# Folding the weights of two layers on four row groups of TensorE, inside a phase of matmuls

## The chip, the cores and the metric

The kernel runs on one core of a Trainium2 chip. The metric is the device time of one execution in microseconds (us). A core has five engines with a queue of instructions each, which they work off in order: TensorE (PE, matmuls), VectorE (DVE), ScalarE (ACT), GpSimd (POOL) and SyncE (SP). DMAs are issued from the queues of SP and POOL here. PE writes to PSUM, whose banks hold 128 partitions of 512 fp32 values; DVE and ACT copy results from there to SBUF.

## What is computed

Four layers follow each other on x, of shape (1024, 16, 16, 16) in fp32 (batch, height, width, channels), each with a group normalisation ahead of it and a residual sum:

```python
x = x + _L0_conv_ref(_gn(x), L0_conv_core0, L0_conv_core1, L0_conv_core2)   # a tensor-train matrix
x = x + _L1_conv_ref(_gn(x), ...)   # a step of a neural cellular automaton
x = x + _L2_conv_ref(_gn(x), L2_conv_filters, L2_conv_bias)                 # a 3x3 convolution
x = x + _L3_conv_ref(_gn(x), ...)   # as layer 1, with other weights
```

Layers 1 and 3 are these, where each channel is filtered with the 3x3 windows `conv1_w` and `conv2_w` and the result goes through two dense layers:

```python
xt = jnp.transpose(x, (0, 3, 2, 1))
pre = _alive(xt)
y1 = _depthwise(xt, conv1_w, conv1_b)
y2 = _depthwise(xt, conv2_w, conv2_b)
flat = jnp.concatenate([xt, y1, y2], axis=1).reshape(B * W * Hh, 48)
h = jax.nn.relu(flat @ fc0_w.T + fc0_b)
d = (h @ fc1_w.T + fc1_b).reshape(B, C, W, Hh)
...
xn = (xt + d) * (pre & _alive(d))
```

The reshape to rows of 48 doesn't move the channels to the end. A row of 48 is therefore three consecutive lines of 16 values of an image plane, some of them from filtered planes. For such lines the kernel doesn't filter the input: it folds the filter into the first dense layer's weights ("weight folding"). The folding depends on weights alone and is done once per execution and layer.

## The kernel before

The batch is cut into two halves of 512, and a matmul works on [128 partitions] x [512 batch columns]. Two buffers of SBUF, X0 and X1, hold one half each of the activations.

**Layer 0** runs in five phases (`layer_train`). A unit of phase 1 has five products of four matmuls each, and every two of these matmuls (L1078) are one piece: ten pieces a unit, 16 units, 160 pieces in the phase. After the first piece of each unit, `build` (L989) makes the stationary weights of the next unit: sixteen passes (L1001) on four row groups into four PSUM banks `pw` of tag "w", of which there are four in all (L1477), and four ACT copies to SBUF (L1006). The products go into three banks of tag "o" and are taken out by DVE (L1112, L1114) and, for one product of a unit, by ACT (L1110). DVE also adds pairs of weights (L1019, "mix").

**Weight folding** (`nca_weights`, L220) makes, for each of layers 1 and 3, a list of steps: inputs, dense0, bias_lines, bias_rows, dense1, taps, order, xpats, and then the folds. Its scratch tiles lie in X1, which is free until the last quarter of the phase.

- `dense0` turns the weights of the first dense layer and stores them to DRAM as `fz`: for each of three lines 18 rows of 128 (the first and last are zero).
- `taps` (L319) collects the filter windows on DVE into `tk`, whose nine used rows stand at partitions 0 to 2, 32 to 34 and 64 to 66, and loads the shifted rows of `fz` from DRAM into `fs` with nine DMAs from POOL (L327). `fs` has 96 partitions and 2,048 columns.
- `order` (L332) spreads `tk` into `tp` with 20 POOL copies (L340) and writes rows of zeros to DRAM (L349, eight DMAs a layer).
- `xpats` (L309) loads, copies and stores another table (L314 to L317) from POOL.
- A fold (L359; eleven a layer) multiplies a column block of `tp` with `fs`, 2,048 columns in four matmuls (L382). `half` does two of them into one bank of tag "m", of which there is one, onto partitions 0 to 35 and 64 to 99, and two copies bring them to a staging tile `fold_e`; `evac` (L149) gives them to ACT and DVE in turn (L152, L154). There are two staging tiles a layer, used in turn. `send` (L390) then writes the fold to DRAM (`wy`) with 2 to 16 DMAs from POOL (L394), 160 in all.

**What sets the order.** The schedule is manual: each engine runs its instructions in the order in which the code issues them. `run` (L1423) issues the pieces of a phase and places background steps between them: a step is issued after the piece at which its planned share of the phase is reached. Here the background is `beside(make1, make3)` over the first 0.74 of phase 1 (L1501): a step of layer 1, a pause of 2.6, the same step of layer 3, a pause of 2.6, and then the pause of the list in L1471. If the pauses take more than 0.7 of the stretch, they are shrunk to that; the rest of the stretch is shared out among the steps:

```python
idle = sum(b[0] for b in bg if b[1] is None) / (us * (hi - lo))
less = min(1.0, 0.7 / idle) if idle else 1.0
```

A step may put instructions on several queues at once, behind all that is already in them. In the last quarter of the phase X1 is loaded for the next phase.

Of the kernel before, what the change touches and what calls it, by code (L numbers as in the profile page):

```python
# [18 lines left out]
B, S, C = 1024, 16, 16  # L19
P = 128  # L20
NB = 512
NCH = B // NB
NL = 32
HID = 128
# [21 lines left out]
TERMS = [  # L46
    ((0, 0),),
    ((0, 1),),
    ((0, 1), (1, 0)),
    ((0, 2), (1, 1)),  # L50
    ((0, 2), (1, 1), (2, 0)),
    ((1, 1), (2, 0)),
    ((1, 2), (2, 1)),
    ((2, 1),),
# [43 lines left out]
def channel(q, k, g):  # L98

    return 12 * q + 3 * ((k - g) % 4) + k  # L100
# [3 lines left out]
def conv_preact_kernel(ctx: ExitStack, tc: tile.TileContext, a: dict, out: bass.AP):  # L104
    nc = tc.nc
    V, A, G, T = nc.vector, nc.scalar, nc.gpsimd, nc.tensor
# [33 lines left out]
    def bank(shape, tag, name):  # L140
        p, sizes = pool["ps"]
        return p.tile(shape, F32, tag=tag, name=name, bufs=sizes[tag])

    def psum(shape, name):
        return bank(shape, shared[0], name)
# [3 lines left out]
    def evac(dst, src):  # L149
        flip[0] ^= 1  # L150
        if flip[0] and not on_vector[0]:
            A.copy(dst, src)  # L152
        else:
            V.tensor_copy(dst, src)  # L154
# [22 lines left out]
    for hf in range(2):  # L177
        rows = slice(64 * hf, 64 * hf + 64)
# [41 lines left out]
    def nca_weights(pre, room):  # L220
# [3 lines left out]
        fz = dram.tile([3, S + 2, HID], F32, tag=pre + "fz", name=pre + "fz")  # L224
# [5 lines left out]
        def tmp(rows, line, lo, n):  # L230
            return flat[0:rows, NB * line + lo : NB * line + lo + n]
# [3 lines left out]
        fc0t, fcb = tmp(16, 1, 0, 3 * HID), tmp(48, 2, 0, 3 * HID)  # L235
        ind = tmp(48, 3, 0, 768).rearrange("p (s r) -> p s r", s=3)

        fs = tmp(96, 5, 0, S * HID)
        tc3 = tmp(96, 2, 384, 96).rearrange("p (j k) -> p j k", k=3)
        tk = tmp(96, 9, 0, 32 * len(TERMS)).rearrange("p (n c) -> p n c", c=32)  # L240
        tp = tmp(96, 14, 0, 72 * len(TERMS)).rearrange("p (n f m) -> p n f m", f=2, m=36)
        pk = tmp(P, 10, 0, 833)
        fold_e = [tmp(P, 12, 0, 2 * NB), tmp(P, 3, 0, 2 * NB)]
        zero = tmp(32, 0, 256, HID)
        def inputs():
            G.dma_start(fc0n, a[pre + "fc0_w"])
            G.dma_start(fc1n, a[pre + "fc1_w"])
            G.dma_start(b0, a[pre + "fc0_b"].unsqueeze(1))
            V.memset(pk[:, 0:512], 0.0)
            V.memset(zero, 0.0)  # L250
            V.memset(ones, 1.0)
            V.memset(cb, 0.0)
            V.memset(ind, 1.0)
            for j in range(2):
                G.dma_start(
                    cb[16 * j + 16 : 16 * j + 32], a[pre + f"conv{j + 1}_b"].unsqueeze(1)
                )
            for m in range(2):
                G.dma_start(pk[16 * m : 16 * m + 16, 512:513], a[pre + "fc1_b"].unsqueeze(1))
            with nc.allow_non_contiguous_dma(reason="144 values"):  # L260
                for j in range(2):
                    for s in range(3):
                        G.dma_start(
                            tc3[32 * s : 32 * s + 3, 16 * j : 16 * j + 16],
                            a[pre + f"conv{j + 1}_w"].rearrange("c o i j -> j c (o i)"),
                        )
            V.memset(tk, 0.0)
            V.memset(tp, 0.0)
            V.memset(fs, 0.0)
            for s in range(3):  # L270
                for base, step in ((s, 1), (15 - s, -1)):
                    G.affine_select(
                        out=ind[:, s], in_=ind[:, s], pattern=[[3 * step, 256]], base=base,
                        channel_multiplier=-16 * step, compare_op=ALU.is_ge, fill=0.0,
                    )
# [43 lines left out]
        def taps():  # L319

            for n, terms in enumerate(TERMS):
                for s, kw in terms:
                    rows = slice(32 * s, 32 * s + 3)
                    V.tensor_copy(tk[rows, n], tc3[rows, :, kw])
            for s in range(3):
                for kh in range(3):
                    G.dma_start(  # L327
                        fs[32 * s + kh : 32 * s + kh + 1],
                        fz[s, 2 - kh : 18 - kh].rearrange("h k -> (h k)").unsqueeze(0),
                    )  # L330

        def order():  # L332

            for f in range(2):
                for k in range(3 - f):
                    for g in range(4):
                        qs = [q for q in (1, 2, 3) if channel(q, k, g) + f >= C]
                        c0 = channel(qs[0], k, g) + f - C
                        col = 12 * k + 4 * (qs[0] - 1) + g
                        G.tensor_copy(  # L340
                            tp[:, :, f, col : col + 4 * len(qs) - 3 : 4],
                            tk[:, :, c0 : c0 + 12 * len(qs) - 11 : 12],
                        )
            for n, pats in enumerate(TRIPLES):
                for i, pat in enumerate(pats):
                    for v in range(2):
                        if pat[v] is None:
                            for s in slots(n, i):
                                G.dma_start(  # L349
                                    wy.rearrange("q g v h s k -> v s (q g) h k")[v, s],  # L350
                                    zero[0:12].unsqueeze(1).broadcast_to([12, S, HID]),
                                )

        def slots(n, i):
            return [6 * k + 3 * n + i for k in range(3)] if n < 2 else [12 + 3 * n + i]
# [3 lines left out]
        def fold(n):  # L359

            steps = []
            for f in range(2):

                uses = []
                for m, pats in enumerate(TRIPLES):
                    for i, pat in enumerate(pats):
                        over = m == 2 and i > 0 or m == 3 and i > 1
                        if over == bool(f):
                            for v in range(2):
                                if pat[v] == n:  # L370
                                    ks = range(3) if m < 2 else [m - 2]
                                    uses += zip(ks, slots(m, i), [v] * 3)
                if not uses:
                    continue
                e = fold_e[turn[0]]
                turn[0] ^= 1

                def half(a2, f=f, e=e):
                    pe = psum([P, NB], pre + "pe")
                    for hh in range(2):  # L380
                        h0 = NB * (2 * hh + a2)
                        T.matmul(  # L382
                            pe[64 * hh : 64 * hh + 36], tp[:, n, f], fs[:, h0 : h0 + NB],
                            start=True, stop=True,
                        )
                    for hh in range(2):
                        rows = slice(64 * hh, 64 * hh + 36)
                        evac(e[rows, NB * a2 : NB * a2 + NB], pe[rows])

                def send(e=e, uses=uses):  # L390
                    for k, s, v in uses:
                        for hh in range(2):
                            r0 = 64 * hh + 12 * k
                            G.dma_start(  # L394
                                wy.rearrange("q g v h s k -> v s (q g) h k")[
                                    v, s, :, 8 * hh : 8 * hh + 8
                                ],
                                e[r0 : r0 + 12].rearrange("p (h k) -> p h k", h=8),
                            )

                steps += [lambda half=half: half(0), lambda half=half: half(1), send]
            return steps

        steps = [inputs, dense0, bias_lines, bias_rows, dense1, taps, order, xpats]
        return L, steps + [x for n in range(len(TERMS)) for x in fold(n)]


# [1061 lines left out]
    def beside(xs, ys):  # L1469

        pause = [12, 8, 1, 1, 6, 6, 4, 4] + [1] * (len(xs) - 8)  # L1471
        return [z for x, y, t in zip(xs, ys, pause) for z in (x, 2.6, y, 2.6, t)]

    L1, make1 = nca_weights("L1_conv_", X1[:, 0:16])
    L3, make3 = nca_weights("L3_conv_", X1[:, 16:32])
    with ExitStack() as es:
        stage(es, dict(gn, w=2, r=2, gq=2, R=1), dict(o=3, w=4, m=1))  # L1477
# [105 lines left out]
```

## Time and profile before

| | |
|---|---|
| median of three runs | 3199.57 us (3197.21 to 3203.37) |
| profiled execution, its own time | 3191.8 us |
| span of the profile | 3190.1 us |
| mean granted TensorE clock | 0.98 of full speed |
| phase 1 of layer 0 in the profile | 234.8 to 601.8 us |
| PE, DVE, ACT, POOL busy in 234.8 to 622 us (387.2 us) | 377.9, 212.3, 69.5, 164.4 us |
| matmul records of the folding (L382) | 176, first at 299.4, last at 517.0 us |

In the lines of the profile an instruction stands as its source line, engine and operation, then what it writes and reads ("out<-in"), with the number of partitions and elements. All scratch tiles of the folding appear as `xn`, since they lie in X1; its PSUM tiles are `L_conv_pe` and the like; its DRAM tables are `L_conv_fz`, `L_conv_wy` and `L_conv_pk`. PEld is TensorE's loading of stationary weights, which overlaps PE. One matmul in fp32 leaves two records, one for each pass. A timeline line gives the start, the time from there to the end of the last of the merged instructions, their number, and in brackets the idle time of the engine before them with what ended it. Ends of matmuls are modelled, so a record's length is longer than its share of PE: what a group costs is read from its start to the start of the next.

### The profile page before, as it was taken

The page shows a single profiled execution, that of the slowest core. Times are in us where ns is not written, and L with a number is a line of the kernel's source. Part 1 is how long each engine was busy: PE and PEld are TensorE (multiplying, and loading weights), DVE is VectorE, ACT ScalarE, POOL GpSimd, SP SyncE. Part 2 cuts the span into 40 slices and gives each one's busy share as a digit, 9 for nine tenths or more (in the row PEclk, how much of TensorE's full clock was granted, in tenths as well). Part 3 has the DMA queues.
Part 4 walks back from the last instruction along what each step waited for, and adds up shares of the span by engine and source line. Part 5 has one row for each costly group of instructions (what it writes and reads, how often), then busy time and mean ns, then how long its engine had stood idle before and what let it go on. Part 6 is the DMA issues. An engine that isn't in the chain of part 4 may idle for free.

```text
span 3190.1 us, 37179 instructions
## 1 busy us (share of the span) xinstructions
PE 3058.5 (96%) x13874; PEld 1260.3 (40%) x13874; DVE 1785.6 (56%) x2378; ACT 1018.3 (32%) x1690; POOL 670.6 (21%) x706
## 2 busy tenths in 40 slices
PE   7899899999999999999999999999979899999996
PEld 5444333444444444444444433333323233333332
DVE  5255345755554555544556678558757647754222
ACT  4331221100001000000111166666624356655553
POOL 1116532200000000000000034435432124432221
PEclk8999999999999999999999999999989999999998
DMA  7535545443333433322222254454476765433445
GB/s 283 201 142 97 121 101 160 133 144 104 104 109 132 146 116 104 104 98 96 90 95 90 76 168 133 129 167 154 139 192 110 185 139 173 136 92 115 128 137 186
DMA packets 243299, 424.77 MB, mean 133 GB/s; under 512 B 37844, under 2 KB 91952, under 8 KB 239408
## 3 DMA queue, kind: packets, MB, share of 16 engines
q1 hardware_dynamic: 217824, 368.63, 35.5%
q0 software_dynamic: 24480, 53.48, 8.3%
q8 instruction: 110, 1.80, 0.2%
q14 instruction: 69, 0.57, 0.1%
q10 hardware_dynamic: 816, 0.30, 0.0%
HBM read 238.78 MB, written 165.60 MB: 127 GB/s over the span
## 4 chain that ended last, share of the span: by engine, by line
issue 46%; PE 31%; POOL 8%; DMA 4%; DVE 2%; SPq 1%; ACT 1%; POOLq 0%; DVEq 0%; ACTq 0%
PE ph L1410 11%; PE po L1078 10%; PE po L1263 4%; POOL res L1313 4%; POOL u L1312 4%; PE po L1160 2%; DMA xn<-xf 1%; PE L_conv_pe L382 1%; SPq L941 1%; DVE xn L621 1%; DMA hx<-xn 1%; PE pw L1001 1%; PE ptout L948 1%; DVE sq L592 1%; POOL L_conv_wy L394 0%
## 5 line engine op out<-in xcount | busy, mean ns | idle before, releaser
L1078 PE MATMUL po<-xn,w 128*128 128x512 f32 x3584 | 1584.3, 598 | 4.6 <-DVE xn L892 4.6
L1078 PEld LDWEIGHTS po<-xn,w 128*128 128x128 f32 x3584 | 669.9, 190 | 852.6 <-issue 833.7
L1413 ACT ACTIVATE hid<-ph,pack 128x512 f32<-128x512 f32 x1024 | 653.9, 686 | 429.2 <-PE ph L1410 308.4
L1114 DVE TENSOR_TENSOR r<-r,po 128x512 f32<-128x512 f32 x576 | 377.8, 683 | 499.0 <-PE po L1078 476.3
L1312 POOL TENSOR_TENSOR u<-u,mask 128x512 f32<-128x512 f32 x128 | 202.5, 1582 | 1858.9 <-DMA nx<-xn 1241.7
L1410 PE MATMUL ph<-xn,wq 32*128 32x512 f32 x3664 | 573.1, 613 | 1.5 <-DMA wq<-L_conv_wy 1.5
L1006 ACT COPY w<-pw 128x512 f32<-128x512 f32 (+1 forms) x320 | 150.6, 558 | 1194.0 <-issue 970.4
L1410 PEld LDWEIGHTS ph<-xn,wq 32*128 32x128 f32 x3664 | 228.6, 184 | 263.3 <-issue 231.4
L1410 PE MATMUL ph<-xn,pack 32*128 32x512 f32 x1288 | 302.2, 631 | 4.5 <-ACT hid L1413 3.2
L1263 PE MATMUL po<-hid,pack 128*32 128x512 f32 x2048 | 283.0, 609 | 1.2 <-DVE u L1275 0.9
L1019 DVE TENSOR_TENSOR w<-w 128x512 f32<-128x512 f32 x320 | 211.2, 684 | 115.2 <-ACT w L1006 114.7
L621 DVE TENSOR_TENSOR xn<-xn,m 128x1024 f32<-128x1024 f32 x160 | 225.9, 1461 | 47.1 <-ACT m L636 47.1
L1313 POOL TENSOR_TENSOR res<-res,u 128x512 f32<-128x512 f32 x128 | 215.2, 1681 | 17.0 <-PE po L1263 2.7
L1275 DVE SCALAR_TENSOR_TENSOR u<-po,pack,xn 128x512 f32<-128x512 f32 x128 | 95.9, 749 | 157.6 <-PE po L1263 150.9
L1160 PE MATMUL po<-xn,convw 128*128 128x512 f32 x368 | 168.5, 609 | 0.0
L1410 PEld LDWEIGHTS ph<-xn,pack 32*128 32x128 f32 x1288 | 114.5, 187 | 100.7 <-issue 61.7
L1114 DVE TENSOR_TENSOR xn<-xn,po 128x512 f32<-128x512 f32 x96 | 64.3, 684 | 125.9 <-PE po L1078 125.8
L592 DVE TENSOR_TENSOR sq<-sq 128x1024 f32<-128x1024 f32 x78 | 110.6, 1418 | 15.2 <-ACT sq L606 12.0
L1263 PEld LDWEIGHTS po<-hid,pack 128*32 128x32 f32 x2048 | 42.9, 108 | 189.7 <-issue 137.4
L394 POOL DMA_DIRECT2D L_conv_wy<-xn x160 | 89.0, 563 | 99.0 <-ACT xn L152 90.7
L1160 PEld LDWEIGHTS po<-xn,convw 128*128 128x128 f32 x368 | 69.3, 193 | 99.3 <-issue 96.7
L592 DVE TENSOR_TENSOR s<-s,xn 128x1024 f32<-128x1024 f32 x60 | 86.4, 1441 | 29.1 <-DMA xn<-xf 27.9
(163 smaller groups left out, 1776.9 us busy)
## 6 DMA issues: line engine op xcount, KB each, us to landing
xf<-r SPq DMA_DIRECT2D x112, 512.0 KB, 3.8
xn<-xf SPq DMA_DIRECT2D x96, 512.0 KB, 5.1
r<-xf SPq DMA_DIRECT2D x80, 512.0 KB, 4.5
wq<-L_conv_wy SPq DMA_DIRECT2D x192, 192.0 KB, 2.8
res<-xf SPq DMA_DIRECT2D x128, 256.0 KB, 3.0
xf<-res SPq DMA_DIRECT2D x96, 256.0 KB, 2.0
res<-xr SPq DMA_DIRECT2D x256, 64.0 KB, 2.8
xf<-conv POOLq DMA_DIRECT2D x64, 256.0 KB, 6.1
```

What stands on the lines that cost most here:

```text
L592: return lambda: V.tensor_tensor(st["t"], st["t"], p(), ALU.add)
L621: V.tensor_tensor(part, part, m().unsqueeze(1).broadcast_to([P, 2, NB]), op)
L1006: A.copy(w[:, k0:4, :, 32 * r : 32 * r + 32].rearrange("p k t (v o) -> p v (k t) o", v=2), pw[r],)
L1019: V.tensor_tensor(w[:, k], w[:, x], w[:, y], ALU.add if sign > 0 else ALU.subtract)
L1078: T.matmul(po, st["w", u][:, matrix, t], x, start=t == 0, stop=t == 3)
L1114: V.tensor_tensor(r[at], r[at], po, ALU.add if sign > 0 else ALU.subtract)
L1160: T.matmul(st["po", h][wh], conv["fw"][:, y], X[:, 16 * wh + h + y - 1], start=y == max(0, 1 - h), stop=y == min(2, S - h),)
L1263: T.matmul(po[32 * j : 32 * j + 32], nca["w1"][:, v], hid[j], start=v == 0, stop=v == 1)
L1312: G.tensor_tensor(u, u, st["m"][:, w2], ALU.mult)
L1313: G.tensor_tensor(r, r, u, ALU.add)
L1410: T.matmul(ph, w, x, start=k == 0, stop=k == len(tiles) - 1)
L1413: A.activation(h, ph, AF.Relu, bias=nca["bt"][:, r : r + 1])
```

## The change

The four matmuls of a fold are placed on the four row groups of TensorE. `fs` now has nine used rows in each of the four groups of 32 partitions, and each group holds one quarter of the 2,048 columns. The DMAs from `fz` keep their number (nine a layer) and write four partitions each. The weights need the same placement: a new tile `tk4` takes, with twelve DMAs a layer from POOL, four copies of the nine rows of `tk`, and `order` spreads `tk4` on 128 partitions in place of `tk` on 96.

A fold is one step (`make`) and no longer two halves. It takes two banks of tag "w", those of `build`, in place of the one of tag "m", and all four copies to the staging tile are on ACT. A layer's list has 30 steps in place of 41.

```diff
-        fs = tmp(96, 5, 0, S * HID)
+        fs = tmp(P, 5, 0, NB)
+        tk4 = tmp(P, 6, 0, 32 * len(TERMS)).rearrange("p (n c) -> p n c", c=32)
+
...
-        tp = tmp(96, 14, 0, 72 * len(TERMS)).rearrange("p (n f m) -> p n f m", f=2, m=36)
+        tp = tmp(P, 14, 0, 72 * len(TERMS)).rearrange("p (n f m) -> p n f m", f=2, m=36)
...
-            V.memset(fs, 0.0)
+            V.memset(tk4, 0.0)
...
             for s in range(3):
+                for g in range(4):
+                    r0 = 32 * g + 3 * s
+                    G.dma_start(tk4[r0 : r0 + 3], tk[32 * s : 32 * s + 3])
                 for kh in range(3):
                     G.dma_start(
-                        fs[32 * s + kh : 32 * s + kh + 1],
-                        fz[s, 2 - kh : 18 - kh].rearrange("h k -> (h k)").unsqueeze(0),
+                        fs[3 * s + kh : 97 + 3 * s + kh : 32],
+                        fz[s, 2 - kh : 18 - kh].rearrange("(g h) k -> g (h k)", g=4),
                     )
...
                             tp[:, :, f, col : col + 4 * len(qs) - 3 : 4],
-                            tk[:, :, c0 : c0 + 12 * len(qs) - 11 : 12],
+                            tk4[:, :, c0 : c0 + 12 * len(qs) - 11 : 12],
...
-                def half(a2, f=f, e=e):
-                    pe = psum([P, NB], pre + "pe")
-                    for hh in range(2):
-                        h0 = NB * (2 * hh + a2)
+                def make(f=f, e=e):
+                    pe = [bank([P, NB], "w", pre + "pe") for _ in range(2)]
+                    for g in range(4):
+                        rows = slice(64 * (g // 2), 64 * (g // 2) + 36)
                         T.matmul(
-                            pe[64 * hh : 64 * hh + 36], tp[:, n, f], fs[:, h0 : h0 + NB],
+                            pe[g % 2][rows], tp[32 * g : 32 * g + 9, n, f], fs[32 * g : 32 * g + 9],
                             start=True, stop=True,
                         )
-                    for hh in range(2):
-                        rows = slice(64 * hh, 64 * hh + 36)
-                        evac(e[rows, NB * a2 : NB * a2 + NB], pe[rows])
+                    for g in range(4):
+                        rows = slice(64 * (g // 2), 64 * (g // 2) + 36)
+                        A.copy(e[rows, NB * (g % 2) : NB * (g % 2) + NB], pe[g % 2][rows])
...
-                steps += [lambda half=half: half(0), lambda half=half: half(1), send]
+                steps += [make, send]
```

## The prediction

> **What bounds the kernel now.** I read the page first: PE is busy for 96% of the span, so what counts is what PE does or waits for. Then I went by the source line of the weight folding, L382, to find when it runs: all of it lies between 299 and 518 us, in the second phase of layer 0 (234.8 to 601.8 us). There I read the timelines of PE, ACT, DVE and POOL.
>
> ```profile
> PE 3058.5 (96%) x13874; PEld 1260.3 (40%) x13874; DVE 1785.6 (56%) x2378; ACT 1018.3 (32%) x1690; POOL 670.6 (21%) x706
> ```
>
> The timeline of PE (start, length, engine, line, count, idle before and its releaser) gives three prices:
>
> ```profile
> 298.36 1.15 PE L1001 MATMUL pw<-R,gq 32*128 32x256 f32 x16
> 299.43 1.05 PE L382 MATMUL L_conv_pe<-xn 96*36 96x512 f32 x4
> 300.42 3.70 PE L1078 MATMUL po<-xn,w 128*128 128x512 f32 x8
> 304.05 1.06 PE L382 MATMUL L_conv_pe<-xn 96*36 96x512 f32 x4
> ...
> 344.77 1.06 PE L382 MATMUL L_conv_pe<-xn 96*36 96x512 f32 x4 [2.13 <-DVE xn L154]
> 345.75 1.98 PE L1078 MATMUL po<-xn,w 128*128 128x512 f32 x4
> 353.62 1.93 PE L382 MATMUL L_conv_pe<-xn 96*36 96x512 f32 x4 [5.89 <-DVE xn L154]
> 355.48 3.78 PE L1078 MATMUL po<-xn,w 128*128 128x512 f32 x4
> 359.19 1.63 PE L1001 MATMUL pw<-R,gq 32*128 32x256 f32 x16
> ...
> 383.83 1.15 PE L1001 MATMUL pw<-R,gq 32*128 32x256 f32 x16
> ...
> 601.80 1.15 PE L1001 MATMUL pw<-R,gq 32*128 32x256 f32 x16
> 602.88 24.30 PE L1078 MATMUL po<-xn,w 128*128 128x512 f32 x56
> ```
>
> An fp32 matmul leaves two records (passes). A pass of 512 columns costs 0.43 us (56 in 24.2). A visit of the folding (one `half`, two column groups at once) holds PE from 299.43 to 300.42, 0.99 us, and the eight passes behind it take 3.63 instead of 3.44: 0.99 + 0.19 = 1.18 us a visit. 44 visits make 51.9 us. On top PE waited for a bank or copy of the fold: 0.44 + 2.13 + 5.89 + 0.49 + 0.40 = 9.35 us, and after the 5.89 ran at about half clock (1.86 for 0.99, 3.71 for 1.91, 1.56 for 1.07: 3.2 us lost).
>
> Who made those waits is seen on ACT and POOL:
>
> ```profile
> 261.99 8.62 POOL L327 DMA_DIRECT2D xn<-L_conv_fz  x18 [0.86 <-DMA L_conv_fz<-xn]
> 281.35 3.85 POOL L340 COPY xn<-xn 96x18 f32<-96x18 f32 x20 [10.74 <-DVE xn L324]
> 285.15 4.82 POOL L349 DMA_DIRECT2D L_conv_wy<-xn  x8
> ...
> 333.07 19.46 POOL L394 DMA_DIRECT2D L_conv_wy<-xn  x35
> ...
> 343.35 0.58 ACT L152 COPY xn<-L_conv_pe 36x512 f32<-36x512 f32 x1 [11.71 <-DMA L_conv_wy<-xn]
> 352.22 0.58 ACT L152 COPY xn<-L_conv_pe 36x512 f32<-36x512 f32 x1 [8.29 <-DMA L_conv_wy<-xn]
> ```
>
> POOL is late: it sends the first fold only from 333.07, and the third fold of each layer may not overwrite its staging tile `fold_e` before that. ACT waits at the head of its queue, and PE behind it. So two things bound this stretch: PE's own work, and once the POOL queue.
>
> **What the Trainium skill says.** "TensorE: Matmul & The Clock Gate", Part 3, says that small matmuls on distinct row groups run at once; the trace agrees (16 builder passes of 256 columns on four row groups in 1.07 us). "TensorEngine Tiling (Array Packing)", Gotcha 1, says that different row tiles cannot access the same PSUM bank at the same time; the trace before has row groups only in separate banks, so it doesn't show this. The Clock Gate page, Part 1, says that an idle window of about 3.4 us halves the clock until a busy one has passed; the 5.89 us wait agrees. "DMA: Bandwidth & Descriptors", Anatomy of one DMA, says that a DMA's semaphore wait stands on the issuing sequencer; the POOL rows agree: one waiting issue holds all behind it.
>
> **The change, part by part.**
>
> *Matmuls.* 88 before, 88 after (22 folds of four), but in 22 visits, not 44. A visit now has eight passes on four row groups: two rounds of 0.43 plus the 0.13 that the visit before had over its two rounds, 0.99, and 0.19 behind it. If all four run at once a visit stays at 1.18 and 22 x 1.18 = 26.0 us go. If groups 0 and 2, which share a bank (as do 1 and 3), take turns, two rounds more: 2.04 a visit. I take 1.18, since they write different partitions, as the two column groups before did at once in one bank.
>
> *Where things are placed.* `run` spreads the steps over 160 pieces (1.72 us each, plus the insertions). With 30 steps a layer instead of 41 the pauses shrink by 0.82 instead of 0.63, so taps of layers 1 and 3 move from pieces 19 and 21 to 26 and 27, order from 23 and 25 to 31 and 33, the first fold from piece 30 to 40. The sum 234.8 + pieces x 1.72 + 1.21 for each builder + 6.6 for the small matmuls of the other steps + 1.18 a visit reproduces the first fold before (31 pieces, four builders: 299.6 against 299.43). After, the first fold comes at 41 x 1.72 + 5 x 1.21 + 6.6 + 234.8 = 318.0.
>
> *POOL.* Taps issue 42 DMAs instead of 18, and the first now copies `tk`, so it waits for the taps copies on DVE. Piece 25 ends at 234.8 + 26 x 1.72 + 3 x 1.21 + 6.6 = 289.8; two L1114 (1.3), a mix (0.7) and half of the fifteen copies (2.38) put POOL's start at 293.2. 42 x 0.48 (L327: 8.62/18; all have few rows) = 20.2, and 0.3 for the wait on four semaphores: order begins at 313.7, not 281.35. Before, the 18 were free: they lay in a 10.74 us wait. What follows is unchanged in count: 333.07 - 281.35 = 51.7 us of order, zero rows, `xpats`. Sends begin at 365.4.
>
> *The wait.* Layer 1's third fold (piece 55, PE at about 353) needs its sends: 365.4 + 10.28 (343.35 - 333.07) = 375.7; layer 3's (piece 56) 365.4 + 19.15 = 384.5. Behind these copies on ACT stand the four builder copies of piece 60. And all four "w" banks are then held by the two folds, so PE stops at the builder of piece 60, at 234.8 + 61 x 1.72 + 6 x 1.21 + 6.6 + 6 x 1.18 = 360.7, plus 3.9 of new waits ahead of it (2 for `tp` of layer 3, ready near 326, and 1.9 for banks), so 364.6. Four copies of 0.58 after 384.5: PE goes on at 387.0. That is a stall of 22 us in one place instead of 9.35 in five. What PE saved or lost before piece 60 is swallowed by it. The same builder stood at 383.83 before.
>
> *From there to 601.80.* Before: 217.97 us, of it 28 visits x 1.18 = 33.0 and waits of 0.9; 184.0 remain. After: 184.0 + 16 visits x 1.18 = 18.9; half clock after the stall, 3.0 (as before; bounds 1.7 to 3.5); and new bank waits. A fold right behind a builder (layer 3's at piece 70, layer 1's at 90) waits for two of the builder's copies, which end 1.3 us after the builder's matmuls (copies of 0.51 us apart); one fold one piece ahead of a builder (69) delays it by 0.5: together 3.1 (bounds 0 and 5). Sum 209.0, so 387.0 + 209.0 = 596.0: 5.8 us earlier. POOL has then 160 x 0.56 = 90 us of sends for 130 us, so no second stall of this kind.
>
> *Cheap edits.* 44 DVE copies of 0.69 become ACT copies of 0.58: DVE is busy for 212 of 387 us in the stage and ACT for 69, so both are hidden, apart from the bank waits above. The memset of `fs` (1.76) becomes one of 288 columns (0.30), hidden under PE. `order` on 128 partitions instead of 96 has the same columns and takes the same time. Nothing later changes in count, so the 5.8 us pass through to the end.
>
> Sum: span 3190.1 - 5.8 = 3184.3. The profiled execution took 3191.8, 7.8 below the median of 3199.57; I take the difference off the median: 3193.8.
>
> **The rivals.**
> - *Shared banks serialise.* In favour: Gotcha 1. Against: column groups of one bank already run at once. Folds before piece 60 hide in the stall; 16 x 0.86 = 13.8 us more: 3207.6, slower. It decides from visits of 1.18 + (5.8 + 6.4)/16 = 1.94 us on.
> - *POOL later still.* If the 24 small copies cost as much as L263's (4.42/6 = 0.74), 24 x 0.26 = 6.2, and if the zero rows meet more traffic, another 2: 8.2 us on PE's restart, one for one: 3202, no measurable change. Against: L263 moves single elements, these whole rows.
> - *POOL earlier.* Of the 51.7 us about 23 are waits, most of them for DMAs of the zero rows and of `xpats`; with half of them gone PE restarts 11 us sooner: 3182.8. Without any stall 22 + 3 us more would go: 3169. Against: the same DMAs meet the same kind of traffic.
>
> **How the numbers follow.** Forecast 3193.8 (own range 3188 to 3200): 0.50. POOL later: 0.18. Shared banks: 0.16. POOL earlier: 0.16. 0.2% is 6.4 us, about what can be told from no change: bounds 3193.2 and 3206.0. The forecast lies almost on the first bound, so 0.23 of its chance counts as faster and 0.27 as same. Faster: 0.23 + 0.16 = 0.39. Same: 0.27 + 0.15 = 0.42. Slower: 0.16 + 0.03 = 0.19. Range 3181 to 3208: both side cases' times are in it, 0.08 lie below and 0.11 above.
>
> **What would show it.** Each visit of the fold about 1.0 us with eight passes; POOL's order copies starting near 314 and its sends near 365; one PE gap of about 22 us ending at 387 before a builder, released by ACT; the builder that stood at 601.80 at 596. Wrong would be a visit of 1.9 us, a PE gap that is much shorter, or a second long gap.

## The result, and the profile after

The changed kernel took 3192.14 us (median of four runs, 3187.84 to 3198.62) beside 3198.39 us (four runs, 3197.07 to 3203.37) for the kernel before on the same chip: a ratio of 0.9979, with a 95% interval of 0.9956 to 1.0003. So it is 0.2% faster or no different. The profiled execution took 3187.84 us with a span of 3186.1, beside 3191.8 and 3190.1 before.

The first line of the page (busy time and instructions of each engine) of the kernel after:

```profile
PE 3041.5 (95%) x13874; PEld 1260.5 (40%) x13874; DVE 1749.5 (55%) x2334; ACT 1041.7 (33%) x1734; POOL 683.2 (21%) x730
```

PE has the same 13874 records and 17 us less busy time, but the span is only 4 us shorter. The timeline of PE after (start, length, engine, line, count, idle before and its releaser) shows where the rest is:

```profile
318.70 1.28 PE L387 MATMUL L_conv_pe<-xn 9*36 9x512 f32 x8 [0.97 <-POOL xn L345]
319.91 3.70 PE L1083 MATMUL po<-xn,w 128*128 128x512 f32 x8
326.75 1.94 PE L387 MATMUL L_conv_pe<-xn 9*36 9x512 f32 x8 [3.14 <-POOL xn L345]
328.62 12.65 PE L1083 MATMUL po<-xn,w 128*128 128x512 f32 x24
341.20 1.06 PE L387 MATMUL L_conv_pe<-xn 9*36 9x512 f32 x8
342.20 1.98 PE L1083 MATMUL po<-xn,w 128*128 128x512 f32 x4
...
347.02 1.59 PE L1006 MATMUL pw<-R,gq 32*128 32x256 f32 x16
...
361.23 7.13 PE L1083 MATMUL po<-xn,w 128*128 128x512 f32 x16
380.38 1.70 PE L1006 MATMUL pw<-R,gq 32*128 32x256 f32 x4 [12.02 <-ACT xn L393]
390.20 2.55 PE L1006 MATMUL pw<-R,gq 32*128 32x256 f32 x12 [8.12 <-ACT xn L393]
392.69 6.18 PE L1083 MATMUL po<-xn,w 128*128 128x512 f32 x8
398.80 1.06 PE L387 MATMUL L_conv_pe<-xn 9*36 9x512 f32 x8
...
417.94 1.54 PE L387 MATMUL L_conv_pe<-xn 9*36 9x512 f32 x8 [0.26 <-ACT w L1011]
...
599.61 1.15 PE L1006 MATMUL pw<-R,gq 32*128 32x256 f32 x16
```

Three things are to be seen. A visit of the fold now has eight passes (x8) and holds PE from 341.20 to 342.20, 1.00 us, as four passes did before. At the builder of piece 60 PE stands twice, for 12.02 and 8.12 us, released by the fold's copies on ACT (L393), and comes out of it at a lower clock (392.69 to 398.80 is 6.11 us for eight passes that took 3.63 before; the granted clock from 390.2 to 398.8 is 0.56 of full speed). And the builder that stood at 601.80 before is at 599.61, only 2.2 us earlier, although a visit with everything behind it is still 1.2 us and there are 22 fewer.

The timelines of POOL and ACT after tell who made the stall:

```profile
292.84 1.99 POOL L330 DMA_DIRECT2D xn<-xn  x4 [31.69 <-DVE xn L326]
...
316.64 3.32 POOL L345 COPY xn<-xn 128x18 f32<-128x18 f32 x20 [1.52 <-DMA xn<-L_conv_fz]
319.91 4.80 POOL L354 DMA_DIRECT2D L_conv_wy<-xn  x8
324.70 3.31 POOL L345 COPY xn<-xn 128x18 f32<-128x18 f32 x20
...
332.71 1.19 POOL L354 DMA_DIRECT2D L_conv_wy<-xn  x2 [1.93 <-DMA L_conv_wy<-xn]
...
339.50 1.06 POOL L316 DMA_DIRECT2D xn<-L_conv_fz  x2 [2.27 <-DMA L_conv_wy<-xn]
...
365.53 6.19 POOL L399 DMA_DIRECT2D L_conv_wy<-xn  x11
372.10 0.56 POOL L399 DMA_DIRECT2D L_conv_wy<-xn  x1 [0.38 <-DMA L_conv_wy<-xn]
374.30 9.44 POOL L399 DMA_DIRECT2D L_conv_wy<-xn  x17 [1.63 <-DMA L_conv_wy<-xn]
385.25 0.56 POOL L399 DMA_DIRECT2D L_conv_wy<-xn  x1 [1.51 <-issue]
```

```profile
378.66 2.15 ACT L393 COPY xn<-L_conv_pe 36x512 f32<-36x512 f32 x4 [27.51 <-DMA L_conv_wy<-xn]
388.48 2.15 ACT L393 COPY xn<-L_conv_pe 36x512 f32<-36x512 f32 x4 [7.67 <-DMA L_conv_wy<-xn]
```

From top to bottom: the DMAs of the taps start at 292.84, `order` at 316.64, the zero rows (L354) at 319.91, the pattern loads (`xpats`, L316 to L319) at 339.50 and the sends (L399) at 365.53. The third folds' copies on ACT wait for those sends until 378.66 and 388.48. From the first zero row to the first send POOL's queue is held again and again by DMAs that have not landed: releasers named DMA stand in the brackets, not engines. These waits add up to 22.7 of the 45.6 us: 10.8 for zero rows, 12.0 within `xpats`, for its own loads and copies. Which of the earlier DMAs an issue waits for, the brackets don't say, and why the first loads of `xpats`, which use nothing of the zero rows, are released by their landing is not shown.

To compare runs below I use one stretch, from the builder at 228.4 us of the profile after to the one at 599.61, which every kernel here has. It is 371.2 us after, 373.4 before; it leaves out what varies ahead of the phase (the same builder stands between 227.1 and 233.6 us in these profiles). A time "on the scale of after" is moved so that this builder stands at 228.4. The runs were made on more than one chip, and the kernel before has a median of 3194.96 to 3197.15 us beside them; each ratio is to the kernel before on the same chip.

### The profile page after: what moved, and what is told of

Same layout as the page of the kernel before. It is cut to its first block, busy times and chain, and to the rows that moved or that the text cites. A ratio compares the mean times of both kernels' runs of the same rounds, so it can differ in the third digit from the quotient of the medians.

```text
span 3186.1 us, 37204 instructions
## 1 busy us (share of the span) xinstructions
PE 3041.5 (95%) x13874; PEld 1260.5 (40%) x13874; DVE 1749.5 (55%) x2334; ACT 1041.7 (33%) x1734; POOL 683.2 (21%) x730
## 4 chain that ended last, share of the span: by engine, by line
issue 52%; PE 24%; POOL 12%; DMA 3%; SPq 1%; DVE 1%; ACT 0%; POOLq 0%; DVEq 0%; ACTq 0%
PE po L1083 9%; PE ph L1415 7%; POOL res L1318 5%; POOL u L1317 5%; PE po L1268 3%; PE po L1165 2%; DMA L_conv_wy<-xn 1%; POOL xf L1197 1%; DMA xn<-xf 1%; PE pw L1006 1%; PE ptout L953 1%; SPq L946 1%; PE L_conv_pe L387 1%; PE po L1174 0%; POOL L_conv_wy L399 0%
## 5 line engine op out<-in xcount | busy, mean ns | idle before, releaser
L1006 PE MATMUL pw<-R,gq 32*128 32x256 f32 (+1 forms) x1280 | 91.2, 385 | 21.1 <-ACT xn L393 20.1
L399 POOL DMA_DIRECT2D L_conv_wy<-xn x160 | 89.2, 565 | 65.1 <-ACT xn L393 54.3
```

What stands on the lines that cost most here:

```text
L1006: T.matmul(pw[r][:, v], st["g", u][rows, v], st["R"][rows, p % 2, 64 * k0 : 256], start=True, stop=True,)
```

## The experiments

My theory at this point: PE's saving is real, but a queue of POOL DMAs ahead of the sends makes PE stand at the builder of piece 60, and the stall swallows the six visits ahead of it and more. The rivals were that the visits themselves give the saving back (a shared bank, more waits for banks), and that PE isn't what sets the pace at all.

**1 and 2: the pattern loads behind the last send.** The same edit in both kernels; `xpats` keeps its place in the list as an empty step, so that no other step moves.

```diff
                 def send(e=e, uses=uses, f=f):
...
+                    if n == 6 and f == 1:
+                        xpats()
...
-        steps = [inputs, dense0, bias_lines, bias_rows, dense1, taps, order, xpats]
+        steps = [inputs, dense0, bias_lines, bias_rows, dense1, taps, order, lambda: None]
```

Changed kernel with it:

> The changed kernel with the steps xpats of both layers issued after the send of the fold n=6, f=1 instead of ahead of the folds; everything else keeps its place. Theory (the gain was given back because POOL's queue is late): the sends start near 338 us instead of 365.5, the third folds find their staging tiles free, and the 20.1 us that PE stood ahead of the builder of piece 60, with some 4 us of half clock, go: span 3186.1 - 24 = about 3162, last builder of the phase near 576 instead of 599.6. Rival (another wait refills the place, for instance the DMAs of the zero rows ahead of the sends): less than 8 us, span above 3178.

Kernel before with it:

> The kernel before with xpats moved in the same way. Theory: PE's waits of 2.13 and 5.89 us and the half clock behind them (3.2 us) go, span 3190.1 - 11 = about 3179. Against it, the changed kernel with xpats moved is then faster by 26.0 us of visits less some 8 us of new waits (banks and tp), about 18 us: that would be what the four row groups are worth once POOL is on time. Rival: the visits are worth no more than the 4 us of the profiles; then both moved kernels differ by 4 us.

Measured: 3169.6 us for the changed kernel (five runs, 3166.63 to 3172.47), a ratio to the kernel before of 0.9916 (0.9903 to 0.9930); 3186.04 us for the kernel before with the move (3181.79 to 3188.32), 0.9965 (0.9951 to 0.9978). Beside the changed kernel's 3192.14 the move is worth 22.5 us, and in the kernel before 11.1 of its 3197.15, near the 24 and 11 that were expected. The sends begin at 341.6 in the first (339.1 on the scale of after) and the stall is gone. POOL's first send, and the builder of piece 60 with what stands around it on PE's timeline:

```profile
341.55 1.17 POOL L399 DMA_DIRECT2D L_conv_wy<-xn  x2 [2.24 <-DMA L_conv_wy<-xn]
```

```profile
328.91 1.94 PE L387 MATMUL L_conv_pe<-xn 9*36 9x512 f32 x8 [2.85 <-POOL xn L345]
...
363.64 7.13 PE L1085 MATMUL po<-xn,w 128*128 128x512 f32 x16
370.70 1.15 PE L1008 MATMUL pw<-R,gq 32*128 32x256 f32 x16
```

Sixteen builder passes in one piece of 1.15 us, no bracket: nothing to wait for. The stretch is 345.4 us, 25.8 less than after. What follows: the stall came from the late sends, and with the stall gone in both kernels the four row groups are worth 16.4 us. The longest wait left in the changed kernel is 2.85 us for the `order` of layer 3.

**3: the fold's input ahead of the taps.** Is it POOL's issue time that makes the sends late?

```diff
         def taps():
+            for s in range(3):
+                for kh in range(3):
+                    G.dma_start(fs[3 * s + kh : 97 + 3 * s + kh : 32], ...)
...
                     G.dma_start(tk4[r0 : r0 + 3], tk[32 * s : 32 * s + 3])
-                for kh in range(3):
-                    G.dma_start(fs[3 * s + kh : 97 + 3 * s + kh : 32], ...)
```

> The changed kernel with the 18 loads of fs issued ahead of the copies of tk, so that they again lie in POOL's wait for DVE. Theory (POOL's queue sets PE's restart one for one): order starts near 307 instead of 316.6, sends near 355.5 instead of 365.5, the restart comes 10 us sooner: span about 3176. Rival (the restart is set by how fast DMAs land, not by POOL's queue): under 3 us.

Measured: 3189.77 us (20 runs, 3185.44 to 3196.02), 0.9978 (0.9971 to 0.9985), which is the changed kernel's own ratio: a miss. POOL's timeline:

```profile
301.27 4.78 POOL L325 DMA_DIRECT2D xn<-L_conv_fz  x9
306.04 5.96 POOL L336 DMA_DIRECT2D xn<-xn  x12
311.99 5.22 POOL L346 COPY xn<-xn 128x18 f32<-128x18 f32 x20
317.16 4.82 POOL L355 DMA_DIRECT2D L_conv_wy<-xn  x8
...
365.13 5.06 POOL L400 DMA_DIRECT2D L_conv_wy<-xn  x9
```

Half of the edit failed by its placing: layer 3's nine loads (301.27) still stand behind layer 1's taps in the queue, because the steps of the layers alternate. But `order` did start 4.7 us earlier than after (311.99 for 316.64) and the sends only 0.4; the builder at 228.4 stands 2.5 us later in this profile, so on the scale of after it is 7.1 and 2.9, and the stretch is 2.8 us shorter (368.4). From the first zero row to the first send it is 48.0 us here and 45.6 after. Something in that stretch isn't paid for by issue time.

**4: a third staging tile.** If the stall is the staging tile's, a third one lets the third fold go without any send.

```diff
-        fold_e = [tmp(P, 12, 0, 2 * NB), tmp(P, 3, 0, 2 * NB)]
+        fold_e = [tmp(P, 12, 0, 2 * NB), tmp(P, 3, 0, 2 * NB), tmp(P, 7, 0, 2 * NB)]
...
-                turn[0] ^= 1
+                turn[0] = (turn[0] + 1) % 3
```

> The changed kernel with a third staging tile for each layer in a free line of the scratch, POOL's queue as it was. Theory: the third folds wait for nothing; the fourth ones need the first sends, which are done at 378.5 and 388.5, and the next builder (piece 70) comes at about 389, so 1 to 2 us of stall are left: gain 22 us, span about 3164, though POOL is as late as before. Rival (the stall only moves to the fourth folds with its length kept): under 5 us.

Measured: 3172.18 us (3168.71 to 3177.08), 0.9920 (0.9902 to 0.9938). The stretch is 351.3 us, 19.9 less than after. POOL is as late as ever (sends at 367.3). The builders of pieces 60 and 70 on PE's timeline:

```profile
370.80 1.15 PE L1006 MATMUL pw<-R,gq 32*128 32x256 f32 x16
...
393.22 1.18 PE L1006 MATMUL pw<-R,gq 32*128 32x256 f32 x4 [0.34 <-ACT xn L393]
395.74 1.90 PE L1006 MATMUL pw<-R,gq 32*128 32x256 f32 x12 [1.34 <-ACT xn L393]
```

PE no longer stands at the builder of piece 60; it waits 0.34 and 1.34 us at the next builder instead, when the fourth folds want the first tile back. So the chain is: late sends, a staging tile that isn't free, the fold's copies on ACT, the banks that these copies empty, and the builder that needs the banks.

**5: every fold visit twice.** The same four matmuls are issued a second time in each visit (`for g in (0, 1, 2, 3, 0, 1, 2, 3)`).

> Every fold visit issues its four matmuls twice over (the second writes the same values again): nothing is left out, 22 visits of eight passes become 22 of sixteen. A visit of eight passes took 1.00 us up to the next instruction's start, a pass 0.43 us in a row group, so the second set costs 2 x 0.43 = 0.86 us where TensorE is what is waited for. My theory: the visits ahead of the stall at the builder of piece 60 are hidden by it (six visits), the sixteen behind it are not, so 16 x 0.86 = 13.8 us: about 3206 beside 3192 of the changed kernel on the same chips. Rival 1: the stall isn't the border and all 22 count, 18.9 us, 3211. Rival 2: something other than TensorE sets the pace behind the stall, and the time stays at 3192.

Measured: 3208.01 us (nine runs, 3201.84 to 3215.66), 1.0031 (1.0018 to 1.0044): 15.9 above the changed kernel. PE's timeline:

```profile
378.93 1.70 PE L1006 MATMUL pw<-R,gq 32*128 32x256 f32 x4 [8.78 <-ACT xn L393]
389.73 2.56 PE L1006 MATMUL pw<-R,gq 32*128 32x256 f32 x12 [9.11 <-ACT xn L393]
...
397.35 1.92 PE L387 MATMUL L_conv_pe<-xn 9*36 9x512 f32 x16
399.20 1.98 PE L1083 MATMUL po<-xn,w 128*128 128x512 f32 x4
```

A visit is 1.85 us instead of 1.00. The six ahead of the stall cost nothing: PE restarts at 389.73 (390.20 after). The sixteen behind it cost 16 x 0.85 = 13.6. The stretch grew by 16.6 (387.8 for 371.2), 3.0 more than the visits; after the bank wait at 467.2 PE ran slower for about 10 us here (a visit took 3.57 us for 1.85; the granted clock from 467 to 480 is 0.63, and 1.00 behind the same wait of the changed kernel). So behind the stall PE sets the pace, and a visit of 1.9 us, as the rival of shared banks had it, would have turned the change into a loss.

**6: the zero rows behind the last send.** The 16 DMAs of L354 become a function `zeros`, called at the end of the layer's last send like `xpats` in the first experiment; `xpats` stays where it was.

> The 16 DMAs that write the zero rows of the folded weights (eight per layer, L354) are moved from the end of `order` to behind the last send of their layer; the pattern loads (L316 to L319) stay ahead of the sends, as in the changed kernel. In the changed kernel's trace the zero DMAs stand from 319.91 to 337.23, and the pattern loads behind them then wait five times for their landing, until 346. My theory after the run with the early fold input: it is the landing of these zero rows that holds POOL's queue, not only their issue. Then the pattern loads start at about 323 and, without those waits, take about 21 us, the sends begin near 344 instead of 365.5, the stall of TensorE at the builder of piece 60 goes nearly whole, and the time falls by about 20 us, to 3172. Rival: only the issue counts, 16 x 0.55 = 8.8 us, so that the sends begin near 357 and the time is about 3183.

Measured: 3161.89 us (3160.16 to 3163.82), 0.9885 (0.9872 to 0.9899), better than expected by 10 us and the fastest kernel of the study. POOL's timeline (the view begins at 318, behind the first seven of the 40 copies) and then PE's:

```profile
317.92 5.44 POOL L345 COPY xn<-xn 128x27 f32<-128x27 f32 x33
323.30 2.90 POOL L316 DMA_DIRECT2D xn<-L_conv_fz  x6
328.02 1.49 POOL L318 DMA_DIRECT2D xn<-xn  x3 [1.81 <-DMA xn<-L_conv_fz]
...
341.35 3.98 POOL L401 DMA_DIRECT2D L_conv_wy<-xn  x7
```

```profile
318.86 1.50 PE L389 MATMUL L_conv_pe<-xn 9*36 9x512 f32 x8 [0.75 <-POOL xn L345]
...
323.92 1.06 PE L389 MATMUL L_conv_pe<-xn 9*36 9x512 f32 x8
...
341.23 1.58 PE L1010 MATMUL pw<-R,gq 32*128 32x256 f32 x16
...
568.92 1.15 PE L1010 MATMUL pw<-R,gq 32*128 32x256 f32 x16
```

The six pattern loads go out in one run, where after they waited five times for a landing, and the sends begin at 341.35. Of the 24.2 us that they are earlier, the 16 issues are worth 16 x 0.6 = 9.6, the waits for zero rows 10.8, and the waits within `xpats`, 8.1 us here for 12.0 after, another 3.9. So landings make up more of it than issues. The expectation had missed a second gain: the `order` copies of layer 3 now follow those of layer 1 at once, and the second fold (323.92) doesn't wait. From the first fold to the builder of piece 50 it is 22.4 us (318.86 to 341.23), 28.3 after (318.70 to 347.02). The stretch is 340.2 us, 31.0 less than after. That is about what stood in the way: 5.9 up to that builder, 23.2 at the builder of piece 60 (368.36 to 392.69 less 1.1 for the builder itself) and 2.5 of slow clock behind it, 31.6.

The span of the profile fell by 24.5, not by 31.0: the start of layer 3's own work is still 29.2 us earlier than after, and the part behind it took 602.8 us for 598.1. The medians differ by 30.3; the profiled execution of after, 3187.84, is the fastest of its four. So the 24.5 holds for these two executions, and why they differ behind the stretch wasn't tried.

**7 and 8: both moves of the first and third experiment together, and two of the four copies on VectorE.**

```diff
-                        A.copy(e[rows, ...], pe[g % 2][rows])
+                        (V.tensor_copy if g % 2 else A.copy)(e[rows, ...], pe[g % 2][rows])
```

Both moves:

> The changed kernel with two moves together: pattern loads behind the last send (3169.6 us when alone) and the 18 loads of the fold's input ahead of the tap DMAs. My theory: with the stall at the builder of piece 60 gone, the wait of the first fold of layer 3 for `order` (2.85 us) is what an earlier `order` can still take away: 3166 to 3167. Rival: the early fold input delays the taps of layer 3, as in the run with it alone, and the wait stays: 3169.6 or a little more.

Both moves and the copies shared out:

> As the kernel with both moves, and of the four copies of a fold visit the two of the second bank go to VectorE instead of ScalarE, so that the pair of banks comes free after two copies of 0.5 us on each engine instead of four on one. My theory: the waits for a bank behind two builders (0.26 and 0.66 us and the slower visits there, about 2.4 us in all) go: about 2 us under the kernel with both moves. Rival: VectorE has its own work in the same stretch, its copies come later than ScalarE's would have, and the time is the same or up to 2 us more.

Measured: 3167.41 us (3166.69 to 3170.21), 0.9904 (0.9891 to 0.9918), and 3172.00 us (3164.09 to 3173.59), 0.9915 (0.9901 to 0.9930). The intervals overlap. The waits behind two builders, 0.26 and 0.66 us in the first, are 0.66 and 0.66 in the second. They are released by the builder's own copies on ACT and not by the fold's, so sharing the fold's copies out didn't shorten them; the stretch is 347.1 us for 345.4. With both moves the wait of 2.85 us is gone, but waits of 0.32, 0.69 and 0.87 us stand at the builder of piece 50 in its place, released by loads of `gq`, the factors from which layer 0's weights are made, and the stretch is no shorter than with the pattern loads moved alone (345.4 us both).

**9: fewer tap DMAs.** This leaves 18 of the 24 DMAs that the change adds out, as its expectation says.

```diff
-                for g in range(4):
+                for g in range(1):
                     r0 = 32 * g + 3 * s
                     G.dma_start(tk4[r0 : r0 + 3], tk[32 * s : 32 * s + 3])
```

> Of the 24 DMAs that copy the taps to the four row groups (L330) only the six for the first row group are left; the taps of the other three row groups stay zero, so the folded weights of three quarters of the rows are zero, while every matmul, copy and send is issued as in the changed kernel. POOL has 18 DMAs of 0.51 us less ahead of `order`, 9.2 us. My theory: what the change puts on POOL is what it gives back, so `order` starts near 307.4, its zero DMAs near 310.7 and the sends near 356; the stall of TensorE at the builder of piece 60 falls from 20.1 to about 11 us and the wait of 3.14 us at layer 3's first fold goes: about 12 us off, 3180. Rival: the sends are held by the landing of the zero rows whenever these start, as in the run with the early fold input, whose `order` was 4.7 us earlier with no gain at the sends: 3189 to 3192.

Measured: 3188.32 us (16 runs, 3182.18 to 3194.31), 0.9980 (0.9973 to 0.9988): the rival's number, and the ratio of the changed kernel itself (0.9979). POOL's timeline:

```profile
314.38 5.19 POOL L345 COPY xn<-xn 128x18 f32<-128x18 f32 x20 [2.76 <-DMA xn<-L_conv_fz]
319.51 4.79 POOL L354 DMA_DIRECT2D L_conv_wy<-xn  x8
...
335.16 0.60 POOL L354 DMA_DIRECT2D L_conv_wy<-xn  x1 [3.40 <-DMA L_conv_wy<-xn]
...
366.72 5.62 POOL L399 DMA_DIRECT2D L_conv_wy<-xn  x10
```

In this profile the builder at 228.4 stands 5.2 us later, so `order` starts at 309.2 on the scale of after, 7.4 earlier, and the sends at 361.5, 4.0 earlier. From the first zero row to the first send it is 47.2 us. PE still stands 8.93 and 6.00 us at the builder of piece 60, and the stretch is 365.0 us, 6.2 less; the times don't show this gain clear of their spread. So the change's own DMAs are a small part of the stall; the stretch between zero rows and sends is the large one, and it doesn't shrink when it starts earlier.

**10: the zero rows moved in the kernel before.**

> The kernel before with its zero-row DMAs (L354 of the changed kernel) moved behind the last send, nothing else. With the same move the changed kernel took 3161.9 us and TensorE had no stall but 0.75 + 0.26 + 0.66 us. My theory: the waits of the kernel before at the builder of piece 60 and behind it go as well, TensorE sets the pace in both, and the difference of the two kernels is then what the four row groups save on TensorE: 44 - 22 visits of 1.18 us = 26.0 less what VectorE, ScalarE and the banks take back; with the pattern loads moved it was 16.4, so 3178, within 3 us. Rival: the four row groups are worth their full 26 us here, 3188.

Measured: 3184.71 us (3182.09 to 3189.81), 0.9968 (0.9958 to 0.9978). That is outside my theory's 3178 within 3 and nearer to the rival's 3188. PE waits only 0.44, 0.49 and 0.40 us for folds, and its stretch is 362.1 us, as with the pattern loads moved (362.1). So the four row groups are worth 362.1 - 340.2 = 21.9 us in the stretch, of the 26.0 estimated for PE. The medians give 3184.71 - 3161.89 = 22.8; they come from two chips, and the two ratios to the kernel before differ by 0.83%, some 26 us, so the times can't tell 22 from 26. The 16.4 of experiments 1 and 2 was smaller, since the changed kernel there still stood for layer 3's `order`: from the first fold to the builder of piece 50 it took 28.5 us (320.93 to 349.44), 6.1 more than in experiment 6, of which 2.85 is the wait and the rest the slower clock behind it (0.77 granted from 328.9 to 343.6).

## Why the prediction came out right, and where it was off

The forecast of 3193.8 us stands beside 3192.14, in the range, and "faster by a little or the same" is what was measured. That the two agree within 1.7 us is partly chance: the forecast took 5.8 us off, the stretch shows 2.2, the two spans differ by 4.0, the two medians by 6.3, and the interval of the ratio reaches from 14 us faster to 1 us slower.

- *The visit.* Forecast 0.99 us for eight passes, measured 1.00. The Trainium skill ("TensorEngine Tiling (Array Packing)", Gotcha 1) says that different row tiles can't access one PSUM bank at the same time; here groups 0 and 2 write one bank, on other partitions, and the visit is no longer than with two groups. The measurement decides: the rival of shared banks falls, and experiment 5 shows what it would have cost.
- *The saving of 26.0 us on PE.* Most of it is there: 21.9 us in the stretch when the zero rows are out of the way in both kernels, 2.2 without that.
- *The placing.* First fold at 318.70 for 318.0, POOL's start at 292.84 for 293.2 (the terms given for it add up to 293.0).
- *The taps.* 42 DMAs took 22.3 us for 20.2 and the landing 1.5 for 0.3, so `order` started 2.9 us late (316.64 for 313.7).
- *Order to sends.* Taken over as 51.7, measured 48.9. The two errors cancel: sends at 365.53 for 365.4.
- *The third folds.* This is the term that was mis-sized: "layer 3's (piece 56) 365.4 + 19.15 = 384.5". The copy was released at 388.48, 22.95 us after the first send, because the sends were held up among themselves: 0.38 and 1.63 us in POOL's timeline by earlier ones that had not landed, and 1.51 us ("issue") for which the profile names no cause. With it PE's restart came at 390.20 for 387.0: 3.2 of the 3.6 us by which the builder at 599.61 missed 596.0.
- *Ahead of the stall.* PE reached the builder of piece 60 at 368.4 for 364.6: the wait for layer 3's `order` was 3.14 us for 2, and the slower clock behind it (0.79 granted from 326.75 to 341.2) was not in the sum. The stall swallowed this, as it swallowed the six visits; PE stood there for 20.1 us and not 22.
- *From there on.* 209.0 us forecast, 209.4 measured (390.20 to 599.61).
- *POOL earlier*, the rival, said 3169 without any stall. Five kernels without the stall gave 3161.9 to 3172.2. What it said of the cause, that about 23 of the 51.7 us are waits, most of them for the DMAs of the zero rows and of `xpats`, fits the changed kernel (22.7 of them), and experiments 1 and 6 show that moving either away ends the stall. *POOL later* hung on the price of the small copies: they took 0.50 to 0.51 us each, not 0.74.

What the forecast, other than its rival, didn't use is that the stall hangs less on the number of DMAs that the change adds (18 of them gone: 6.2 us of the stretch) than on the 16 zero rows that were there before (moved: 31.0).

## What to carry to other kernels

When a faster engine saves time ahead of a wait whose end it doesn't set, the wait takes it back: ask first for the next fixed release behind the saving, here the staging tile, and count only the work behind it. POOL's queue of DMAs had to be priced by landings as well as by issues (14.6 and 9.6 us of the 24.2 by which the sends came earlier in experiment 6). What isn't needed soon (tables of zeros, patterns for a later layer) belongs behind what releases a buffer, as the moves of experiments 1 and 6 show here. With 16 such DMAs moved in both kernels, the four row groups take 21.9 us off the stretch, where alone they took 2.2; the change and the move together make the kernel 1.15% faster.

## What the runs showed of the hardware that wasn't expected

The zero rows land slowly. The DMA view of after, from 320 to 340 us:

```profile
q0 software_dynamic: 580, 1.23, 82.8%
...
L_conv_wy<-xn POOLq DMA_DIRECT2D x16, 96.0 KB, 11.1
```

The columns of the first line are the queue, packets, MB and share of the 16 engines' time, those of the second the issues, their size and the median time to landing. The DMA engines are busy for 82.8% of these 20 us with POOL's queue alone and move 1.23 MB, 62 GB/s; a zero-row DMA of 96 KB lands after 11.1 us. The Trainium skill ("DMA: Bandwidth & Descriptors", Anatomy of one DMA) gives 2.0 us plus the bytes over 436 GB/s for one DMA from GpSimd, for 96 KB an estimate of 2.2; here eight of them go out within 4.80 us, and it is five times that. The sends, 48 KB each to the same table, land after 2.4 us in the same kernel (365 to 400 us). Why these writes are slow was not tried.

The zero rows go together with delays on another queue. In experiment 3, four loads of `gq` issued from SP (SPq is SP's DMA queue) fall among the zero rows (317.16 to 336.31), and their issuing takes 20.35 us where the next four take 3.40:

```profile
322.50 20.35 SPq L990 DMA_DIRECT2D gq<-g_dram  x4
...
347.16 3.40 SPq L990 DMA_DIRECT2D gq<-g_dram  x4
```

In the four experiments with an earlier `order` (3, 7, 8 and 9) PE waits 1.3 to 1.9 us for these loads at the builder of piece 50; in the changed kernel it doesn't. That the zero rows are the cause was not tried.

A wait of 20 us on PE cost more than itself: the 12 passes behind it took 2.49 us, where 16 take 1.07, and the next eight 6.11 for 3.63. The granted clock is 0.50 of full speed from 390.2 to 397 and 1.00 from 398.
